# Window attention's norms and inverse roots: another division of work among the engines

## The chip, the cores and the metric

The kernel runs on one core of a Trainium2 chip. The metric is device time in microseconds (us) for one execution. The core's engines work side by side, each through its own queue in order: TensorE (PE in the profile; PEld are its weight loads), VectorE (DVE), ScalarE (ACT), GpSimd (POOL) and SyncE (SP), whose queue issues nearly all DMAs. They wait for each other through semaphores. All data is float32.

## What is computed

Two layers on an image batch x of 8 x 192 x 64 x 64, one behind the other. The first widens to 384 channels, convolves 3 x 3 by channel, runs a gated scan in four directions, normalises and returns to 192 channels. The second is attention in windows of 8 x 8 pixels with six heads of 32 channels, and an MLP. The change is in the second; its core, cut:

```python
def _layer_norm(x, g, b):
    mu = jnp.mean(x, -1, keepdims=True)
    var = jnp.mean(jnp.square(x - mu), -1, keepdims=True)
    return (x - mu) * jax.lax.rsqrt(var + EPS_LN) * g + b      # EPS_LN = 1e-5
...
shortcut = _layer_norm(xs, norm1_g, norm1_b)
...
qkv = (xin @ qkv_w.T + qkv_b).reshape(B_, N, 3, HEADS, HEAD_DIM)
...
attn = jnp.einsum('bhnd,bhmd->bhnm', _l2n(q), _l2n(k)) * temperature
kth = jax.lax.top_k(attn, IN_CC)[0][..., -1:]
attn = jnp.where(attn >= kth, attn, NEG)
...
attn = jax.nn.softmax(attn + rpb[None], axis=-1)
out = jnp.einsum('bhnm,bhmd->bhnd', attn, v)
...
out = out @ proj_w.T + proj_b
...
x2 = shortcut + out
hdn = _layer_norm(x2, norm2_g, norm2_b)
hdn = jax.nn.gelu(hdn @ fc1_w.T + fc1_b, approximate=False) @ fc2_w.T + fc2_b
x2 = x2 + hdn
```

The residual is the normalised input: the sum behind the attention adds `shortcut` (`xin` is its window layout), not the layer's input. `_l2n` divides by the length of a vector. So each token needs three inverse square roots: of the variance at the first norm, of the squared lengths of q and k (twelve heads' worth), and of the variance at the second norm.

## The kernel before

**Tiling.** An image is cut into 8 rows of windows ("window rows", `g`) of 8 x 64 = 512 tokens, and these into four blocks of 128 tokens, tokens on partitions, 192 channels along the free axis. There are 64 window rows in all (8 images of 8). The first layer works on 384 channels as three tiles (`ct`) of 128 partitions and, in the scan, on 512 pixels at each of 8 steps `t`, for 4 directions and 3 channel tiles: 12 tiles a step.

**Order.** The kernel does not issue in the order of its source. Generators write down steps (`plan(engine, cost, function, r=..., w=...)`), each with an estimated cost and the tiles it reads and writes. `Plan.order` then simulates the queues `RUNS` times, moving each step's rank towards the time when its result is needed, and keeps the shortest of these schedules. `SLACK` (ns) is how late an input may be for a step to be still picked by its rank. The engines' queues are filled in the chosen order, which is fixed from then on. Three strands lie side by side: `front` (first layer's convolution of the next image), `scan` (of this image), `window_row` (attention of the image before). The first image's convolution runs ahead of the plan, from a separate piece of code (lines 477 to 502), and the attention of the last image can start only when its scan and the statistics behind it are done (`scales`, line 1135).

**A window row** (line 1141 on): `zg` is loaded and scaled (1171); `tokens` (1186) multiplies it with `w_out`, whose columns have been freed of their mean, so that its result needs no mean for the first norm. VectorE multiplies by the gain `n1_g` into `s0` (1193), ScalarE sums the squares (1205), POOL scales and adds epsilon (1211), and `rsqrt` (613 to 620) makes the inverse root: Ln, Exp and Square on ScalarE, then a Newton step of three POOL instructions. This happens for two blocks at a time, twice a row. ScalarE scales `s0` (1219), PE transposes it into `sT` (1151), and from `sT` come q, k (1236) and v (1275). `nn` holds the squared lengths; it has the same `rsqrt` (one call for all four blocks) and scales q and k (1310). Scores, the search for the top entries, the mask and the softmax follow (1351 to 1437).

Behind the attention, again for two blocks at a time, `projected` (1506) multiplies with `w_pr`; VectorE adds `s0` (1518) and takes mean and variance with batch-norm instructions (1529, 1530); POOL adds epsilon (1536), `rsqrt` follows, and `less_m` = -mean x root is made on ScalarE and POOL (1546, 1553). ScalarE writes the normalised `xn` (1561), PE transposes it (1574, 1576), and the MLP follows: `widened` (1593, 1597), Gelu (1613), `narrowed` (1627).

**Other lines that are spoken of.** `scales` (1130 to 1135) is a run of tiny VectorE instructions on tiles of SBUF behind each image's scan. The mask (1392) and the scaling of q and k (1310) are VectorE instructions with two inputs in SBUF. GpSimd's large instructions in the scan are lines 896, 913, 917, 928, 981, 987 and 989.

## Time and profile before

| | |
|---|---|
| three runs | 7535.86, 7552.91, 7554.57 us; median 7552.91 |
| profiled execution | 7551.0 us; span of its instructions 7549.2 us |
| busy: PE, DVE, POOL, ACT | 6680.5 (88%), 6360.6 (84%), 6227.8 (82%), 4895.1 us (65%) |
| mean granted TensorE clock | 0.864 of full speed |
| end of the images' scans (line 1135) | 955, 1822, 2663, 3549, 4439, 5337, 6188, 7036 us |
| Gelu instructions before the scan's last gate instruction | 54 of 64 |

"Busy" is the time in which an engine had an instruction in work, also when that instruction stood still for something inside it. In a group's line the numbers behind the bar are the group's busy time in us and the mean of one instruction in ns, then the engine's idle time ahead of the group with what ended it. In a timeline a line gives start and duration in us. The DMA share is 0.2 to 0.6 in all stretches.

### The profile page before, as it was taken

The numbers are of one execution on the slowest core, as the hardware profiler recorded it, in microseconds if no ns is written. First come the engines' busy times: TensorE is split into PE (matmuls) and PEld (weight loads), VectorE is DVE, ScalarE is ACT, GpSimd is POOL, SyncE is SP. The second block draws the span as 40 slices with busy tenths as digits, with TensorE's granted clock in tenths as the row PEclk, the third lists the DMA queues.
The fourth block names the chain that finished last, engine by engine and source line by source line (L and its number), as shares of the span: only waits on it lengthen the run. The fifth ranks groups of instructions, "written<-read, shape, count | busy, mean of one in ns | idle before, by whom it ended". The sixth has DMA issues, their size and how long they took to land. (4 is left out here: it accounts for less than half of the span.)

```text
span 7549.2 us, 141750 instructions
## 1 busy us (share of the span) xinstructions
PE 6680.5 (88%) x50180; PEld 3448.8 (46%) x50180; DVE 6360.6 (84%) x15477; ACT 4895.1 (65%) x9649; POOL 6227.8 (82%) x6333
## 2 busy tenths in 40 slices
PE   7888799898989899888999899989888888898887
PEld 3333344444444444444445444444444444444554
DVE  6787798988899889898898988889899988899543
ACT  3555377765676567675777757776666656666765
POOL 1898788998899989987988888889899989899422
PEclk8887699987988889898988889987888878888999
DMA  5666354313541246213641144411121121111110
GB/s 165 163 174 162 108 154 124 81 50 100 157 120 50 68 133 158 65 49 94 162 117 44 53 121 132 119 47 53 54 55 48 45 67 44 50 45 45 32 22 14
DMA packets 988330, 669.39 MB, mean 89 GB/s; under 512 B 651971, under 2 KB 814214, under 8 KB 987622
## 3 DMA queue, kind: packets, MB, share of 16 engines
q1 hardware_dynamic: 986486, 658.87, 32.5%
q8 instruction: 398, 6.52, 0.4%
q14 instruction: 310, 2.54, 0.1%
q10 hardware_dynamic: 1136, 1.47, 0.1%
HBM read 433.98 MB, written 226.18 MB: 87 GB/s over the span
## 5 line engine op out<-in xcount | busy, mean ns | idle before, releaser
L808 PE MATMUL g<-xe,w_g 32*128 32x512 f32 x3648 | 1165.2, 749 | 228.5 <-DVE dx L967 80.5
L808 PE MATMUL g<-xo,w_g 32*128 32x512 f32 x3648 | 1201.7, 730 | 186.3 <-DVE dx L967 95.6
L865 ACT ACTIVATE ab<-g 128x512 f32<-128x512 f32 x1344 | 784.9, 596 | 397.9 <-PE nb L808 169.6
L896 POOL TENSOR_TENSOR ab<-ab 128x512 f32<-128x512 f32 x672 | 866.0, 1289 | 163.1 <-ACT ab L865 151.5
L928 POOL TENSOR_TENSOR pw<-pw,rr 128x512 f32<-128x512 f32 x672 | 865.9, 1289 | 134.7 <-ACT rr L911 113.7
L913 POOL TENSOR_TENSOR pw<-pw,pq 128x512 f32<-128x512 f32 x672 | 881.6, 1312 | 77.7 <-DVE pq L872 52.0
L917 POOL TENSOR_TENSOR pw<-pw,pq 128x512 f32<-128x512 f32 x672 | 877.4, 1306 | 15.5
L909 ACT ACTIVATE rr<-nb,eps 128x512 f32<-128x512 f32 x672 | 461.9, 687 | 577.9 <-DVE nb L906 575.3
L981 POOL TENSOR_TENSOR dx<-dx,hu 128x512 f32<-128x512 f32 x576 | 743.0, 1298 | 111.0 <-DVE hu L972 94.2
L808 PEld LDWEIGHTS g<-xo,w_g 32*128 32x128 f32 x3648 | 412.8, 207 | 726.8 <-DVE dx L967 200.3
L808 PEld LDWEIGHTS g<-xe,w_g 32*128 32x128 f32 x3648 | 407.2, 212 | 702.9 <-DVE dx L967 179.4
L1627 PE MATMUL lp<-hd,w_f 128*64 128x256 f32 (+1 forms) x2304 | 604.7, 502 | 57.2 <-ACT hd L1613 15.0
L989 POOL TENSOR_TENSOR y<-y,dx 128x512 f32<-128x512 f32 x384 | 598.2, 1565 | 2.2
L695 PE MATMUL lp<-strip,w_cv 128*32 128x256 f32 x8064 | 566.8, 420 | 27.3 <-DMA strip<-pad 22.7
L924 DVE SCALAR_TENSOR_TENSOR nb<-nb,rr 128x512 f32<-128x512 f32 x672 | 464.0, 691 | 145.4 <-ACT rr L911 142.8
L933 DVE SCALAR_TENSOR_TENSOR nb<-nb,pw 128x512 f32<-128x512 f32 x672 | 463.6, 690 | 139.3 <-POOL pw L928 137.4
L906 DVE TENSOR_TENSOR nb<-nb,ab 128x512 f32<-128x512 f32 x672 | 464.1, 691 | 115.1 <-POOL ab L896 106.6
L972 DVE TENSOR_TENSOR hu<-g,hid 128x512 f32<-128x512 f32 x768 | 516.8, 678 | 0.9 <-PE g L808 0.6
L887 ACT ACTIVATE nb<-nb 128x512 f32<-128x512 f32 x672 | 399.5, 595 | 141.1 <-DVE pq L874 80.3
L808 PE MATMUL nb<-xe,w_g 32*128 32x512 f32 x672 | 479.1, 799 | 10.0 <-DVE hid L941 9.8
L808 PE MATMUL nb<-xo,w_g 32*128 32x512 f32 x672 | 464.1, 777 | 16.9 <-DVE hid L941 16.8
L941 DVE TENSOR_TENSOR hid<-lx,nb 128x512 f32<-128x512 f32 x672 | 454.2, 676 | 4.9
(223 smaller groups left out, 16413.8 us busy)
## 6 DMA issues: line engine op xcount, KB each, us to landing
strip<-pad SPq DMA_DIRECT2D x1008, 132.0 KB
xd<-xsT SPq DMA_DIRECT2D x384, 256.0 KB
x<-xs SPq DMA_DIRECT2D x64, 768.0 KB
xd<-xs SPq DMA_DIRECT2D x192, 256.0 KB
z<-y SPq DMA_DIRECT2D x64, 768.0 KB
zg<-z SPq DMA_DIRECT2D x64, 768.0 KB
pad<-xin SPq DMA_DIRECT2D x168, 264.0 KB
xsT<-sn SPq DMA_DIRECT2D x168, 256.0 KB
```

The lines of the kernel that those rows point to most:

```text
L695: nc.tensor.matmul(pc()[q * RG : (q + 1) * RG, k * 256 : (k + 1) * 256].rearrange("p (h w) -> p h w", h=4), lhsT=w_cv[:, ct, q, dx, :], rh ...
L808: nc.tensor.matmul(dst, lhsT=w[rows, col : col + P], rhs=xp[rows, :], start=True, stop=True)
L865: lambda r=r: nc.scalar.activation(ab()[:, r, :], g[r](), AF.Abs),
L896: plan("POOL", gp(512), lambda: nc.gpsimd.tensor_add(ab()[:, 0, :], ab()[:, 0, :], ab()[:, 1, :]), w=[ab])
L906: plan("DVE", vec(512), lambda: nc.vector.tensor_add(nb(), nb(), ab()[:, 0, :]), r=[ab], w=[nb])
L913: plan("POOL", gp(512), lambda: nc.gpsimd.tensor_add(one(), one(), pq()[:, 0, :]), r=[(pq, 0)], w=[pw])
L917: lambda: nc.gpsimd.tensor_add(one(), one(), pq()[:, 1, :]),
L928: plan("POOL", gp(512), lambda: nc.gpsimd.tensor_mul(one(), one(), rr()), r=[rr], w=[pw])
L972: lambda: nc.vector.tensor_mul(like(hu(), d), like(pu(), d), state(d, ct)),
L981: plan("POOL", gp(512), lambda: nc.gpsimd.tensor_add(dx(), dx(), hu()), r=[hu], w=[dx])
L989: nc.gpsimd.tensor_add(y, y, dx().rearrange("p (c i) -> p i c", c=CH))
L1627: nc.tensor.matmul(dst[:, at : at + rhs.shape[-1]], lhsT=lhsT, rhs=rhs, **flags)
```

## The change

The text of the changed parts, cut (unchanged neighbours as context):

```diff
-    RUNS = 60
-    SLACK = 40.0
+    RUNS = 9
+    SLACK = 20
...
-                s.rank = (s.rank + rank) / 2 if n else rank
+                s.rank = 0.4 * s.rank + 0.6 * rank if n else rank
...
-        by_vector = [(ct, u) for ct, u in units if ct < CT - 1 or u == 0]
+        by_vector = [(ct, u) for ct, u in units if ct < CT - 1]
...
-            if n in (4, 6, 7):
-                convolved_by_products(CT - 1, (4, 6, 7).index(n) + 1)
+            if n in (2, 4, 5, 6):
+                convolved_by_products(CT - 1, (2, 4, 5, 6).index(n))
```

```diff
-    def rsqrt(v, key, shape, name, gain=1.0):
+    def rsqrt(v, key, shape, name, gain=1.0, mean=1.0, eps=0.0):
...
-        plan("ACT", tiny, lambda: nc.scalar.activation(r(), v(), AF.Ln), r=[key], w=[r])
+        more = {"bias": {1e-5: eps5}[eps]} if eps else {}
+        plan("ACT", tiny, lambda: nc.scalar.activation(r(), v(), AF.Ln, scale=1.0 / mean, **more), r=[key], w=[r])
         plan("ACT", tiny, lambda: nc.scalar.activation(r(), r(), AF.Exp, scale=-0.5, bias=log_c[gain]), w=[r])
-        plan("ACT", tiny, lambda: nc.scalar.activation(sq(), r(), AF.Square), r=[r], w=[sq])
+        plan("ACT", tiny, lambda: nc.scalar.activation(sq(), r(), AF.Square, scale=mean**-0.5), r=[r], w=[sq])
         def newton():
-            nc.gpsimd.tensor_mul(v(), v(), sq())
-            nc.gpsimd.tensor_scalar(v(), v(), -1.0, 3.0 * c * c, ALU.mult, ALU.add)
-            nc.gpsimd.tensor_mul(v(), v(), r())
+            nc.vector.scalar_tensor_tensor(v(), v(), eps * mean, sq(), ALU.add, ALU.mult)
+            nc.vector.scalar_tensor_tensor(v(), v(), 3.0 * c * c, r(), ALU.subtract, ALU.mult)
-        plan("POOL", (750.0, 60.0), newton, r=[r, sq], w=[key])
+        plan("DVE", (160.0 + 4 * math.prod(shape[1:]) / 0.96, 85.0), newton, r=[r, sq], w=[key])
```

The root comes out with its sign turned; the weights that follow it (`w_qk`, `w_v`, `w_f1`, and `w_dg` below) are turned too, once, ahead of the plan. The gain `n1_g` goes into `w_qk` and `w_v` there as well, so `s0` and `sT` hold the norm without its gain, and the multiplication of line 1193 becomes a ScalarE copy:

```diff
             plan(
-                "DVE",
-                vec(2 * DM),
-                lambda two=two, pz=pz: nc.vector.tensor_mul(
-                    s0()[:, two, :],
-                    pz()[:, 0 : 2 * DM].rearrange("p (k m) -> p k m", k=2),
-                    n1_g.unsqueeze(1).to_broadcast([P, 2, DM]),
+                "ACT",
+                act(2 * DM),
+                lambda two=two, pz=pz: nc.scalar.copy(
+                    s0()[:, two, :], pz()[:, 0 : 2 * DM].rearrange("p (k m) -> p k m", k=2)
                 ),
...
-            plan(
-                "POOL",
-                tiny,
-                lambda ss=ss: nc.gpsimd.tensor_scalar(ss(), ss(), 1.0 / DM, 1e-5, ALU.mult, ALU.add),
-                w=[ss],
-            )
-            rsqrt(ss, ss, [P, 2], "ss")
...
+        rsqrt(ss, ss, [P, NT], "ss", mean=DM, eps=1e-5)
```

Behind the attention the residual is added by TensorE into the same PSUM bank, from `sT` with the small diagonal matrix `w_dg` (96 x 97, the gain on its diagonal, and a column that yields minus the mean); `w_pr` has a 193rd column for the mean, too. ScalarE copies the sum out, takes minus the mean, and sums the squares of what is left:

```diff
+                    for j in range(2):
+                        cols = slice(at + j * HALF, at + j * HALF + more)
+                        nc.tensor.matmul(pp()[:, cols], lhsT=sT[:, j, tok], rhs=w_dg[:, j, :], start=False, stop=j == 1)
...
+            def unfolded(t2=t2, pp=pp):
+                nc.scalar.copy(
+                    x2()[:, 2 * t2 : 2 * t2 + 2, :].rearrange("p k (j m) -> p k j m", j=2),
+                    bass.AP(pp().tensor, pp().offset, [pp().ap[0], [DM + 1, 2], [HALF + 1, 2], [1, HALF]]),
+                )
+            plan("ACT", act(2 * DM), unfolded, r=[pp], w=[(x2, t2)])
...
+                lambda pp=pp, two=slice(2 * t2, 2 * t2 + 2): nc.scalar.copy(less_m()[:, two], view(pp(), [[DM + 1, 2]], HALF)),
...
+            def spread(t2=t2):
+                for k in range(2 * t2, 2 * t2 + 2):
                     nc.scalar.activation(
-                        xn()[:, tt, :], x2()[:, tt, :], AF.Identity, bias=less_m()[:, k : k + 1], scale=sd()[:, k : k + 1]
+                        xn()[:, k, :], x2()[:, k, :], AF.Square, bias=less_m()[:, k : k + 1], accum_out=sd()[:, k : k + 1]
                     )
...
+        rsqrt(sd, sd, [P, NT], "sd", mean=DM, eps=1e-5)
+        plan("DVE", (70.0, 85.0), lambda: nc.vector.tensor_mul(less_m(), less_m(), sd()), r=[sd], w=[less_m])
```

The batch-norm instructions, the addition of line 1518 and the POOL steps of lines 1536 and 1553 are gone. Each of the two norms now has one root for all four blocks of a window row, where it had two for two blocks each. `sT` is kept twice (by the row's parity), since it is read until the projection; `s0`, `st` and `acc_p` have one buffer where they had two. No DMA is added or taken away, but for the shapes of three small loads.

More of the change, by code (lines that the diff above doesn't have):

```diff
@@ L387, in tile_ss2d_then_window_attention @@
     w_pr = load("w_pr", rows=P)
-    n1_g = load("n1_g", a["n1_g"].partition_broadcast(P))
+    n1_g = load("n1_g")
     n1_b = load("n1_b")
@@ L413, in tile_ss2d_then_window_attention @@
     xT = blank("xT", [P, 2, GT])
-    sT, oT = (blank(n, [P, 2, GT], 0.0) for n in ("sT", "oT"))
-    for t in (sT, oT):
+    sTs, oT = [blank(f"sT{k}", [P, 2, GT], 0.0) for k in range(2)], blank("oT", [P, 2, GT], 0.0)
+    w_dg = blank("w_dg", [P, 2, HALF + 1], 0.0)
+    for t in (*sTs, oT):
         nc.gpsimd.memset(t[HALF : HALF + 1, 1, :], 1.0)
@@ L482, in convolved_by_products @@
         def convolved_by_products(ct, u):
-            acc = epool.tile([P, 16, W], F32, name="acc_p", bufs=2)
+            acc = epool.tile([P, 16, W], F32, name="acc_p", bufs=1)
             for k in range(2):
@@ L559, in tile_ss2d_then_window_attention @@
         bias_row("b_pr", w_pr, [(b_v[:, j : j + 1], w_pr[0:HALF, j, :]) for j in range(2)], "n1_br")
+        msum = prep.tile([P, 2], F32, name="msum")
+        nc.vector.tensor_reduce(msum, w_pr, AX.X, ALU.add, negate=True)
+        nc.vector.tensor_scalar(w_pr[:, :, HALF], msum, 1.0 / DM, None, ALU.mult)
+        for j in range(2):
+            own, mean = (slice(0, HALF), HALF) if j == 0 else (slice(1, HALF + 1), 0)
+            gain = n1_g[:, j : j + 1]
+            nc.vector.tensor_scalar(gain, gain, -1.0, None, ALU.mult)
+            nc.vector.tensor_scalar(w_dg[0:HALF, j, own], ident[0:HALF, 0:HALF], gain, None, ALU.mult)
+            nc.vector.tensor_scalar(w_dg[0:HALF, j, mean : mean + 1], gain, -1.0 / DM, None, ALU.mult)
+            for w in (w_qk[0:HALF, j, :], w_v[0:HALF, j, :]):
+                nc.vector.tensor_scalar(w, w, gain, None, ALU.mult)
         ps = prep_ps.tile([P, 512], F32, name="ps_pre")
@@ L570, in tile_ss2d_then_window_attention @@
             w = w_f1[:, ci, :]
-            nc.vector.tensor_scalar(w, w, n2_g[:, ci : ci + 1], None, ALU.mult)
+            nc.vector.tensor_scalar(w, w, n2_g[:, ci : ci + 1], -1.0, ALU.mult, ALU.mult)
         top_b = prep.tile([P, 3], F32, name="top_b")
@@ L704, in convolve @@
             rows = slice(s * 64, (s + 1) * 64)
-            st = Held(fpool, [P, CH, 64], "st", bufs=2)
+            st = Held(fpool, [P, CH, 64], "st", bufs=1)
             plan(
@@ L1114, in scan @@
         rsqrt(gr, gr, [P, CT], "gr")
-        plan("DVE", tiny, lambda: nc.vector.tensor_mul(gn(), gn(), gr()), r=[gr], w=[gn])
+        plan("DVE", tiny, lambda: nc.vector.scalar_tensor_tensor(gn(), gn(), -1.0, gr(), ALU.mult, ALU.mult), r=[gr], w=[gn])
         pg = bank()
@@ L1153, in turn @@
                         )
-                plan("PE", turned(4), turn, r=[src], w=[pt])
+                plan("PE", turned(4), turn, r=[src], w=[pt, (key, "room")])
                 plan(
@@ L1162, in two_blocks @@
                 )
+        sT, kS = sTs[g % 2], f"sT{g % 2}"
         zg = Held(lpool, [P, CT, CH, 64], "zg", bufs=1)
@@ L1173, in window_row @@
         plan("ACT", (2116.0, 102.0), scaled_up, r=[sc, bb], w=[zg])
-        s0 = Held(lpool, [P, NT, DM], "s0", bufs=2)
+        s0 = Held(lpool, [P, NT, DM], "s0", bufs=1)
+        ss = Held(small, [P, NT], "ss")
         for t2 in range(2):
             pz = bank()
-            ss = Held(small, [P, 2], "ss")
             for k in range(2):
@@ L1200, in window_row, with squares, scaled @@
             )
-            def squares(pz=pz, ss=ss):
+            def squares(t2=t2, pz=pz):
                 for k in range(2):
                     part = pz()[:, k * DM : (k + 1) * DM]
-                    nc.scalar.activation(part, part, AF.Square, accum_out=ss()[:, k : k + 1])
-            plan("ACT", (782.0, 100.0), squares, w=[pz, ss])
-            plan(
-                "POOL",
-                tiny,
-                lambda ss=ss: nc.gpsimd.tensor_scalar(ss(), ss(), 1.0 / DM, 1e-5, ALU.mult, ALU.add),
-                w=[ss],
-            )
-            rsqrt(ss, ss, [P, 2], "ss")
-            def scaled(t2=t2, ss=ss):
-                for k in range(2):
-                    part = s0()[:, 2 * t2 + k, :]
+                    at = 2 * t2 + k
+                    nc.scalar.activation(part, part, AF.Square, accum_out=ss()[:, at : at + 1])
+            plan("ACT", (782.0, 100.0), squares, w=[pz, (ss, t2)])
+            yield
+        rsqrt(ss, ss, [P, NT], "ss", mean=DM, eps=1e-5)
+        for t2 in range(2):
+            def scaled(t2=t2):
+                for k in range(2 * t2, 2 * t2 + 2):
+                    part = s0()[:, k, :]
                     nc.scalar.activation(part, part, AF.Copy, scale=ss()[:, k : k + 1])
             plan("ACT", (694.0, 106.0), scaled, r=[ss], w=[(s0, t2)])
-            yield
+        yield
         plan.lane = 7
-        two_blocks(sT, "sT", s0)
+        two_blocks(sT, kS, s0)
         yield
@@ L1238, in projected @@
                     )
-            plan("PE", mm(2, DIN), projected, r=["sT"], w=[pq, (qk, "room")])
+            plan("PE", mm(2, DIN), projected, r=[kS], w=[pq, (qk, "room")])
             plan(
@@ L1281, in values @@
                         )
-            plan("PE", mm(4, DM), values, r=["sT"], w=[pv, (v, "room")])
+            plan("PE", mm(4, DM), values, r=[kS], w=[pv, (v, "room")])
             plan(
@@ L1496, in window_row @@
         x2, xn = (Held(lpool, [P, NT, DM], n, bufs=1) for n in ("x2", "xn"))
+        less_m, sd = Held(small, [P, NT], "less_m"), Held(small, [P, NT], "sd")
         for t2 in range(2):
@@ L1499, in window_row, with projected @@
             two = slice(2 * t2, 2 * t2 + 2)
-            stats, mv, sd = Held(small, [P, 2, 6], "stats"), Held(small, [P, 2, 2], "mv"), Held(small, [P, 2], "sd")
-            def projected(t2=t2, pp=pp):
+            more = HALF + 1
+            def projected(t2=t2, pp=pp, sT=sT):
                 for k in range(2):
                     tok = slice((2 * t2 + k) * P, (2 * t2 + k + 1) * P)
+                    at = k * (DM + 1)
                     for j in range(2):
                         nc.tensor.matmul(
-                            pp()[:, k * DM : (k + 1) * DM],
-                            lhsT=oT[:, j, tok],
-                            rhs=w_pr[:, j, :],
-                            start=j == 0,
-                            stop=j == 1,
-                        )
@@ L1514, in window_row @@
-            plan("PE", mm(4, DM), projected, r=["oT"], w=[pp, (x2, "room"), (xn, "room")])
-            plan(
-                "DVE",
-                vec(2 * DM),
-                lambda two=two, pp=pp: nc.vector.tensor_add(
-                    x2()[:, two, :].rearrange("p k m -> p (k m)"),
-                    pp()[:, 0 : 2 * DM],
-                    s0()[:, two, :].rearrange("p k m -> p (k m)"),
-                ),
-                r=[pp, s0],
-                w=[(x2, t2)],
-            )
@@ L1527, in moments @@
-            def moments(t2=t2, stats=stats, mv=mv):
-                for k in range(2):
-                    nc.vector.bn_stats(stats()[:, k, :], x2()[:, 2 * t2 + k, :])
-                    nc.vector.bn_aggr(mv()[:, k, :], stats()[:, k, :])
-            plan("DVE", (947.0, 83.0), moments, r=[(x2, t2)], w=[stats, mv])
-            plan(
-                "POOL",
-                tiny,
-                lambda mv=mv, sd=sd: nc.gpsimd.tensor_scalar(sd(), mv()[:, :, 1], 1e-5, 1.0, ALU.add, ALU.mult),
-                r=[mv],
-                w=[sd],
-            )
@@ L1540, in window_row @@
-            rsqrt(sd, sd, [P, 2], "sd")
-            less_m = Held(small, [P, 2], "less_m")
+                            pp()[:, at : at + DM + 1], lhsT=oT[:, j, tok], rhs=w_pr[:, j, :], start=j == 0, stop=False
+                        )
+                    for j in range(2):
+                        cols = slice(at + j * HALF, at + j * HALF + more)
+                        nc.tensor.matmul(pp()[:, cols], lhsT=sT[:, j, tok], rhs=w_dg[:, j, :], start=False, stop=j == 1)
+            plan("PE", mm(6, 2 * (DM + HALF + 2) / 3), projected, r=["oT", kS], w=[pp, (x2, "room"), (xn, "room")])
@@ L1545, in window_row, with normed @@
                 tiny,
-                lambda mv=mv, less_m=less_m: nc.scalar.activation(less_m(), mv()[:, :, 0], AF.Copy, scale=-1.0),
-                r=[mv],
-                w=[less_m],
-            )
-            plan(
-                "POOL",
-                tiny,
-                lambda sd=sd, less_m=less_m: nc.gpsimd.tensor_mul(less_m(), less_m(), sd()),
-                r=[sd],
-                w=[less_m],
-            )
-            def normed(t2=t2, less_m=less_m, sd=sd):
-                for k in range(2):
-                    tt = 2 * t2 + k
-                    nc.scalar.activation(
-                        xn()[:, tt, :], x2()[:, tt, :], AF.Identity, bias=less_m()[:, k : k + 1], scale=sd()[:, k : k + 1]
+                lambda pp=pp, two=slice(2 * t2, 2 * t2 + 2): nc.scalar.copy(less_m()[:, two], view(pp(), [[DM + 1, 2]], HALF)),
+                r=[pp],
+                w=[(less_m, t2)],
+            )
+            def spread(t2=t2):
+                for k in range(2 * t2, 2 * t2 + 2):
+                    nc.scalar.activation(
+                        xn()[:, k, :], x2()[:, k, :], AF.Square, bias=less_m()[:, k : k + 1], accum_out=sd()[:, k : k + 1]
+                    )
+            plan("ACT", (782.0, 100.0), spread, r=[(x2, t2), (less_m, t2)], w=[(xn, t2), (sd, t2)])
+            yield
+        rsqrt(sd, sd, [P, NT], "sd", mean=DM, eps=1e-5)
+        plan("DVE", (70.0, 85.0), lambda: nc.vector.tensor_mul(less_m(), less_m(), sd()), r=[sd], w=[less_m])
+        for t2 in range(2):
+            def normed(t2=t2):
+                for k in range(2 * t2, 2 * t2 + 2):
+                    nc.scalar.activation(
+                        xn()[:, k, :], x2()[:, k, :], AF.Identity, bias=less_m()[:, k : k + 1], scale=sd()[:, k : k + 1]
                     )
             plan("ACT", (890.0, 95.0), normed, r=[(x2, t2), less_m, sd], w=[(xn, t2)])
-            yield
+        yield
         for ci in range(2):
@@ L1698, in _laid_out @@
     cols = lambda a, n: np.ascontiguousarray(a.reshape(-1, n).T)
+    gap = lambda a: np.concatenate([a[..., :HALF], np.zeros_like(a[..., :1]), a[..., HALF:]], -1)
     L0, L1 = "L0_conv_", "L1_conv_"
@@ L1740, in _laid_out @@
         "b_v": cols(qkv_b[2].reshape(DM), HALF),
-        "w_pr": rows(proj.reshape(DM, DM), HALF),
-        "b_pr": f(L1 + "proj_b").reshape(1, DM),
-        "n1_g": f(L1 + "norm1_g"),
-        "n1_br": f(L1 + "norm1_b").reshape(1, DM),
+        "w_pr": gap(rows(proj.reshape(DM, DM), HALF)),
+        "b_pr": gap(f(L1 + "proj_b").reshape(1, DM)),
+        "n1_g": cols(f(L1 + "norm1_g"), HALF),
+        "n1_br": gap(f(L1 + "norm1_b").reshape(1, DM)),
         "n1_b": cols(f(L1 + "norm1_b"), HALF),
```

## The prediction

> **What bounds the kernel now.** I read first the busy times by stretch, cut where the eight batches end (a batch ends with its line 1135, at 955, 1822 ... 7036 us), then the chain of waits, then the groups of instructions, last the instructions of single lines.

> ```profile
> core 0: us, PE busy (x) PEld busy (x) DVE busy (x) ACT busy (x) POOL busy (x), PEclk, DMA share, GB/s
> ...
> 4439.00:5337.00 898.00, 821.93 (x6494) 432.23 (x6490) 787.47 (x1922) 606.40 (x1205) 777.31 (x787) 0.87 0.35 92
> 5337.00:6188.00 851.00, 743.97 (x5156) 396.30 (x5156) 781.39 (x1927) 564.51 (x1139) 778.87 (x789) 0.84 0.19 52
> 6188.00:7036.00 848.00, 731.19 (x5237) 391.05 (x5238) 763.39 (x1986) 571.34 (x1172) 749.01 (x785) 0.86 0.17 47
> 7036.00:7549.00 513.00, 432.09 (x3961) 273.64 (x3959) 225.47 (x1134) 323.39 (x688) 146.62 (x317) 0.92 0.09 20
> ```

> The reader is to see three engines level. In the sixth scanned batch DVE and POOL are busy 92% each and PE 87%; in the one before, which also has the next batch's convolution, PE is at 92%. Only behind 7036, where the last attention rows run alone, is PE far ahead of the rest. ACT is never above 70%.

> ```profile
> PE 8%; DVE 7%; POOL 4%; ACT 4%; issue 1%; DMA 0%; SPq 0%; POOLq 0%; ACTq 0%; DVEq 0%
> ```

> The chain can be followed back to 5780 us. Adding its pieces up by engine, from 5780 to 7036 they are DVE 34.0%, PE 25.2%, POOL 21.7%, ACT 12.1%; from 7036 on PE 50%, ACT 27%, DVE 15%, POOL 5%. I use these shares as weights: work added to an engine lengthens its stage by the share times the engine's growth. This assumes that the last batch and a half stand for all, a choice that I come back to.

> **The change, part by part.** VectorE loses four groups (their busy time is the first number behind the bar):

> ```profile
> L1193 DVE TENSOR_TENSOR s<-lp,n_g 128x384 f32<-128x384 f32 x128 | 69.6, 545 | 11.4 <-PE lp L1186 11.4
> L1518 DVE TENSOR_TENSOR x<-lp,s 128x384 f32<-128x384 f32 x128 | 69.6, 545 | 33.6 <-PE lp L1506 33.5
> L1529 DVE BATCH_NORM_STATS2 stats<-x 128x6 f32<-128x192 f32 x256 | 86.5, 338 | 0.6
> L1530 DVE BATCH_NORM_AGGREGATE mv<-stats 128x2 f32<-128x6 f32 x256 | 46.5, 182 | 8.9
> ```

> 272 us, 4.25 us for each of 64 rows. It gains seven small operations a row: two Newton steps for each of ss, sd and nn, and less_m times sd. They read two tensors of SBUF, and what such an operation costs here depends on GpSimd:

> ```profile
> 1816.44 1.18 DVE L1131 TENSOR_TENSOR sc<-sc,vecs 128x3 f32<-128x3 f32 x1
> 1817.66 1.45 DVE L1132 TENSOR_SCALAR sc<-sc 128x3 f32<-128x3 f32 x1
> 1819.14 1.43 DVE L1133 TENSOR_TENSOR bb<-sc,vecs 128x3 f32<-128x3 f32 x1
> ...
> 1816.33 1.27 POOL L913 TENSOR_TENSOR pw<-pw,pq 128x512 f32<-128x512 f32 x1
> 1817.55 3.00 POOL L989 TENSOR_TENSOR y<-y,dx 128x512 f32<-128x512 f32 x2
> ```

> Three elements take 1.2 to 1.45 us, and each ends within 0.1 us of a POOL instruction's end. With POOL idle the same line takes 0.164 us (its shortest of eight). Big ones show it too: line 1392 has a median of 0.97 us in the last two scanned batches and 0.66 behind 7036, where POOL rests; line 1310 2.23 against 1.76. The removed four have a PSUM operand or a single input and show no such wait.

> So the price, from rows: the first of a run takes 0.17 plus the mean excess of 1392 and 1310, 0.39: 0.56 us. One that follows at once meets a POOL instruction just begun: mean of lines 1131 to 1134, 0.96 us. A row has three firsts and four followers, 3 x 0.56 + 4 x 0.96 = 5.5 us while a scan runs, and 7 x 0.17 = 1.2 us behind the last scan. 56 x 5.5 + 8 x 1.2 + 12 (the same steps for gr, eight times) = 330 us; net **+58 us, +0.9%** of DVE's 6360.6. Bounds: all bare, 80 us, net -192 (-3.0%); all as line 1132 (1.16), 484 us, net +212 (+3.3%). I stay between, as POOL is busy some 90% of a batch.

> [...]

> POOL loses lines 618 to 620 (for ss 82.9, sd 76.9, nn 52.1 us), 1211 (26.0), 1536 (28.1), 1553 (25.4) and gr's (5): **-296 us, -4.75%**. VectorE's waits for ScalarE's Square now stand in VectorE's queue (51 us of idle time in POOL's before), with the scan's products queued behind them and PE waiting for these; against that go the 55 us of idle time ahead of the removed DVE groups. I set the two equal.

> TensorE gains, per row, eight products w_dg x sT of 97 columns, each two passes: 16 passes. A pass of 192 columns (line 1506, 16 in 2.87 us) takes 179 ns, one of 128 columns behind a 128-column load (line 1627, x2 against ident, 8 in 1.05 us) 131. The load does not shrink with 97 columns, so I take 131, with 99 (scaled by columns) and 179 as bounds: 16 x 0.131 = 2.1 us a row, **+134 us, +2.0%** (1.5 to 2.7%). The 193rd column of the other products is nothing. [...]

> ScalarE gains four copies of 384 columns (line 1287: 485 ns), four squares with a sum (between 509, line 1205 with its accumulator read, and 728, line 1561's 536 plus the same read; 728, as they too read SBUF and a bias), and loses six small operations (203, 292, 201 ns, twice): 1.94 + 2.91 - 1.39 = 3.5 us a row, **+221 us, +4.5%** (3.4% with 509).

> Weighted over the stretch from 955 to 7036 (6081 us): 0.340 x 0.9 - 0.217 x 4.75 + 0.252 x 2.0 + 0.121 x 4.5 = +0.34%, **+20 us**.

> Start: VectorE does nine convolution units of 11.3 us in a row (0.81 + 8 x 1.3, up to 116.5 us), now eight; the ninth goes to PE and ACT, which idle there. The folding of the norm's gain adds some 3 us of small operations behind it: **-8 us**. If acc_p's single buffer holds PE up, that is hidden by the units left. st's single buffer makes a ScalarE copy wait for the store before; copies are 14.9 us apart in the median, so I count nothing (up to 5 us).

> Order: 54 of the 64 Gelu instructions stand before the scan's last gate instruction on ScalarE; in the new order 56 do. Two rows move into scanned batches. Behind 7036 nine rows' worth cost PE 48, DVE 25, ACT 36, POOL 16 us each; with the terms above (and 1.4 us of port waits on lines 1392 and 1310) 50, 27.6, 39.4 and 11.7, weighted 29 us: **+59 us** for two. At the end, the first row of the last batch needed 140 us from line 1171 to its Gelu (7037 to 7177), two older rows among it, and seven more came 50.4 us apart. Without the older rows I take 125 (105 to 140), and 1.3 us more a row by the end's weights: -15 + 10 = **-5 us**. x2's chain there loses its wait for the moments and gets the sum of squares instead.

> Sum: -8 + 20 + 59 - 5 = +66 us on the profiled 7551.0 us, which lies 2 below the median: **7617 us**.

> **Rivals.** *GpSimd's relief decides (faster).* In the stretch from 955 to 7036 POOL, freer by 4.75%, lets the seven operations through bare: DVE -3.0%, weighted sum -1.0%, -61 us, and the two rows fit into what came free: 7551 - 61 - 8 - 5 = 7477. For it: 193 of DVE's 652 us of idle time between 1000 and 7000 us end on POOL. Against it: POOL would still be busy over 85%. It decides where the seven average below 0.3 us (0.79 in my sum): 56 x 7 x 0.49 x 0.34 = 65 us is what the forecast lies above the old time.

> *VectorE or TensorE alone sets the pace (much slower).* All seven at 1.16 us, wholly on the path: 7551 + 212 - 8 = 7755. Or PE: 56 x 2.1 + 2 x 48 - 8 - 5 = +201, 7752. For it: PE's 92% with the convolution; DVE ends most of PE's idle time (337 of 603 us in the same stretch). Against PE: its granted clock rises where it is fuller (0.94 at 95% busy from 2750 to 3000 us, 0.73 at 76% from 750 to 1000), so filled gaps pay part.

> *It does not do what it says.* What moves is the planner's order (9 rounds for 60, slack 20 for 40), which knows nothing of the port; works added and taken cancel: 7551, give or take 20.

> **How the numbers follow.** Forecast 0.45 (7575 to 7700), GpSimd 0.28 (7400 to 7540), one engine alone 0.14 (7700 to 7800), cancelling 0.13. The three runs before lie 0.25% apart, so 0.3%, 23 us, is what can be told from no change. Faster 0.30, same 0.13, slower 0.57. Range 7430 to 7770, the forecast's own 7575 to 7700.

> **What would show it.** The two Newton lines and less_m's product: right if they average 0.6 to 1.1 us before the last batch ends and under 0.25 behind it; wrong below 0.3. POOL's busy sum near 5930, PE's near 6810, ACT's near 5115, DVE's near 6410. Passes w_dg x sT near 131 ns apart. First DVE work behind the convolutions 11 us earlier. Last batch's end near 500 us from its scales. It is wrong if the batches, with eight rows each, take less than 850 us.

## The result, and the profile after

The changed kernel takes 7593.74 us in the median of five runs (7579.65 to 7601.64), the kernel before 7548.15, also of five (7535.86 to 7554.57): a ratio of 1.0056, interval 1.004 to 1.0072. That is 46 us slower. The profiled execution took 7583.05 us, 32 more than the one before.

The busy times by stretch, with the same columns as before, cut at the ends of the last scanned batches (6271 and 7132 us):

```profile
core 0: us, PE busy (x) PEld busy (x) DVE busy (x) ACT busy (x) POOL busy (x), PEclk, DMA share, GB/s
5392.00:6271.00 879.00, 761.36 (x5492) 411.35 (x5491) 801.78 (x1889) 587.89 (x1214) 743.24 (x618) 0.85 0.18 51
6271.00:7132.00 861.00, 740.25 (x5452) 405.30 (x5450) 779.77 (x1950) 602.54 (x1225) 719.24 (x601) 0.87 0.17 46
7132.00:7581.00 449.00, 379.69 (x3488) 246.47 (x3488) 187.88 (x960) 298.55 (x656) 91.22 (x112) 0.93 0.10 21
```

Before, VectorE and GpSimd stood level at 92% in the first of these stretches. Now GpSimd is at 85% and VectorE still at 91%, in a stretch 28 us longer. The page's chain of waits says the same; it now reaches back over some 35% of the span, and VectorE leads it:

```profile
DVE 13%; PE 11%; ACT 5%; POOL 3%; issue 2%; DMA 1%; ACTq 0%; SPq 0%; DVEq 0%; POOLq 0%
```

The new groups of VectorE, with the mean of one instruction in ns behind the comma:

```profile
L630 DVE SCALAR_TENSOR_TENSOR nn<-nn,nn_r 128x48 f32<-128x48 f32 x64 | 54.6, 854 | 2.2
L630 DVE SCALAR_TENSOR_TENSOR ss<-ss,ss_r 128x4 f32<-128x4 f32 x64 | 50.3, 786 | 2.2
L630 DVE SCALAR_TENSOR_TENSOR sd<-sd,sd_r 128x4 f32<-128x4 f32 x64 | 50.3, 786 | 2.2
L629 DVE SCALAR_TENSOR_TENSOR sd<-sd,sd_q 128x4 f32<-128x4 f32 x64 | 48.6, 759 | 45.9 <-ACT sd_q L626 45.8
...
L629 DVE SCALAR_TENSOR_TENSOR nn<-nn,nn_q 128x48 f32<-128x48 f32 x64 | 37.3, 583 | 13.6 <-ACT nn_q L626 8.2 <-POOL at L1443 3.8 <-POOL pw L938 1.0
L629 DVE SCALAR_TENSOR_TENSOR ss<-ss,ss_q 128x4 f32<-128x4 f32 x64 | 36.4, 569 | 17.0 <-ACT ss_q L626 17.0
L1547 DVE TENSOR_TENSOR less_m<-less_m,sd 128x4 f32<-128x4 f32 x64 | 30.8, 481 | 0.4
```

Together these seven groups are 308 us for 448 instructions on four or 48 elements. A timeline of VectorE, and of GpSimd at the same time (start and duration in us), shows one row's three:

```profile
6625.06 0.59 DVE L629 SCALAR_TENSOR_TENSOR sd<-sd,sd_q 128x4 f32<-128x4 f32 x1 [1.43 <-ACT sd_q L626]
6625.68 1.44 DVE L630 SCALAR_TENSOR_TENSOR sd<-sd,sd_r 128x4 f32<-128x4 f32 x1
6627.15 1.19 DVE L1547 TENSOR_TENSOR less_m<-less_m,sd 128x4 f32<-128x4 f32 x1
...
6624.32 1.30 POOL L927 TENSOR_TENSOR pw<-pw,pq 128x512 f32<-128x512 f32 x1
6625.56 1.53 POOL L999 TENSOR_TENSOR y<-y,dx 128x512 f32<-128x512 f32 x1
6627.04 1.28 POOL L938 TENSOR_TENSOR pw<-pw,rr 128x512 f32<-128x512 f32 x1
```

Each of the three ends when the GpSimd instruction beside it ends: 6625.65 beside 6625.62, 6627.12 beside 6627.09, 6628.34 beside 6628.32. The loss has this shape, but the same trace shows gains too. By stage, from the scales' times and the first instruction of the plan on PE:

| stage | before, us | after, us | difference |
|---|---|---|---|
| start, to the plan's first matmul | 132.7 | 123.1 | -9.6 |
| first scan, no attention beside it | 822.9 | 809.8 | -13.1 |
| seven scans with attention beside them | 6080.4 | 6198.8 | +118.4 |
| after the last scan | 513.2 | 449.6 | -63.6 |

The last two lines have not the same work in them: of the 64 window rows' Gelus, 54 start before the end of the last scan in the kernel before and 56 in the changed one, so two rows have moved from the last line to the one above it, as forecast.

### The profile page after: what moved, and what is told of

Its sections match the earlier page's. It is cut to its first block, busy times and chain, and to the rows that moved or that the text cites. A ratio compares the mean times of both kernels' runs of the same rounds, so it can differ in the third digit from the quotient of the medians.

```text
span 7581.3 us, 142641 instructions
## 1 busy us (share of the span) xinstructions
PE 6741.8 (89%) x51240; PEld 3534.1 (47%) x51240; DVE 6430.6 (85%) x15176; ACT 5030.1 (66%) x10035; POOL 5952.7 (79%) x4968
## 5 line engine op out<-in xcount | busy, mean ns | idle before, releaser
L818 PE MATMUL g<-xo,w_g 32*128 32x512 f32 x3648 | 1164.5, 725 | 200.2 <-DVE dx L977 98.5
L818 PE MATMUL g<-xe,w_g 32*128 32x512 f32 x3648 | 1121.2, 732 | 184.1 <-DVE dx L977 55.9
L818 PEld LDWEIGHTS g<-xo,w_g 32*128 32x128 f32 x3648 | 393.2, 205 | 716.1 <-DVE dx L977 196.4
L1618 PE MATMUL lp<-hd,w_f 128*64 128x256 f32 (+1 forms) x2304 | 644.2, 532 | 59.8 <-ACT hd L1604 50.0
L989 POOL TENSOR_TENSOR y<-hu,dx 128x512 f32<-128x512 f32 x192 | 245.1, 1285 | 307.1 <-DVE hu L982 174.5
L1618 PEld LDWEIGHTS lp<-hd,w_f 128*64 128x64 f32 (+1 forms) x2304 | 293.9, 184 | 408.5 <-issue 246.2
```

The lines of the kernel that those rows point to most:

```text
L818: nc.tensor.matmul(dst, lhsT=w[rows, col : col + P], rhs=xp[rows, :], start=True, stop=True)
L1618: nc.tensor.matmul(dst[:, at : at + rhs.shape[-1]], lhsT=lhsT, rhs=rhs, **flags)
```

## The experiments

Two theories stood against each other: that the small two-input operations stand still on VectorE and this gives the gain back, and that TensorE's and ScalarE's added work, or the planner's settings, make the loss. In kernels marked "same order" every instruction stands where it stood in the plan. Each ratio is to the kernel before as it ran beside that experiment (medians of 7549 to 7558 us), so a difference in us between two experiments is uncertain by some 10 us.

**The second SBUF input, taken away.** e4 puts the root and its square into a PSUM bank:

```diff
-        r, sq = Held(small, shape, name + "_r"), Held(small, shape, name + "_q")
+        both, n = bank(), math.prod(shape[1:])
+        tall = lambda k: both()[:, 64 * k : 64 * k + n].rearrange("p (a b) -> p a b", a=shape[1]) if len(shape) == 3 else both()[:, 64 * k : 64 * k + n]
+        r, sq = (lambda: tall(0)), (lambda: tall(1))
...
```

> The changed kernel with the root and its square (outputs of Exp and Square) in a PSUM bank, so that each Newton instruction on VectorE has one input in SBUF and one in PSUM, same count; planned anew. Theory (the wait is for the second SBUF input): the six groups fall from 0.57-0.85 to about 0.2 us each, DVE busy by about 200 us, the time by 65-95 us to 7500-7530, less what the bank costs the others (0-40 us). Rival (the wait is for GpSimd by any small VectorE instruction, or only their number counts): the groups stay above 0.5 us, time 7580-7620.

Measured 7551.05 us, ratio to the kernel before 1.0001 (0.9992 to 1.0011): 43 us less than the changed kernel. The answers for its two Newton lines, with shortest, median and longest duration in ns:

```profile
L631 DVE SCALAR_TENSOR_TENSOR ss<-ss,lp x64: 105/147/159, 962.3 to 7372.6; 128x4 f32<-128x4 f32 x64
L631 DVE SCALAR_TENSOR_TENSOR sd<-sd,lp x64: 128/148/160, 1114.7 to 7500.3; 128x4 f32<-128x4 f32 x64
...
L632 DVE SCALAR_TENSOR_TENSOR ss<-ss,lp x64: 157/158/160, 962.4 to 7372.8; 128x4 f32<-128x4 f32 x64
L632 DVE SCALAR_TENSOR_TENSOR nn<-nn,lp x64: 203/203/206, 1001.2 to 7424.7; 128x48 f32<-128x48 f32 x64
```

None is longer than 206 ns, where the changed kernel's reach 3770. Same engine, same count, same arithmetic; only one input has left SBUF. In e4, 294 of the 400 Newton instructions begin while a GpSimd instruction is in work and end over 60 ns before it does; of the changed kernel's 464 small operations (the 448 and gr's 16) 3 do. That the wait belongs to the second SBUF input is shown. The gain is below the 65 to 95 us expected, by less than the 40 us allowed for the bank, and this kernel was planned anew, so not all of the 43 us need be the wait's.

**Two-input operations, doubled.** e5 and e6, same order, add two unused VectorE instructions behind each Newton step (`spare` is a small SBUF tile; the line that makes it is not shown):

```diff
+            for k in range(2):                                        # e5
+                nc.vector.scalar_tensor_tensor(spare[:, 2 + k], spare[:, 0], 0.5, spare[:, 1], ALU.add, ALU.mult)
+            for k in range(2):                                        # e6
+                nc.vector.reciprocal(spare[:, 2 + k], spare[:, 0])
```

> The changed kernel, same order, and behind each Newton step two more VectorE products of two small SBUF tensors that nothing uses (400 more in all). Theory (each stands still for GpSimd's current instruction): 0.7-0.9 us each, DVE busy +280 to +350, the time by the weights 0.34-0.46 up by 100 to 170, to 7695-7765. Rival (only the number of instructions counts): as e6.

> As e5, with two reciprocals of one small tensor in place of the products. Theory: about 0.2 us each without a wait, DVE busy +70 to +90, 7615-7645. Rival (only the number counts): the same time as e5.

e5 took 7740.92 us, ratio 1.0243 (1.0228 to 1.0258), e6 7618.94, ratio 1.0079 (1.0063 to 1.0094): 147 and 25 us more than the changed kernel for the same number of instructions. First e5's, then e6's:

```profile
L633 DVE SCALAR_TENSOR_TENSOR spare<-spare x400: 147/155/1591, 931.1 to 7704.6; 128x4 f32<-128x4 f32 x134
```

```profile
L633 DVE RECIPROCAL spare<-spare x400: 137/157/175, 929.0 to 7579.5; 128x4 f32<-128x4 f32 x134
```

The same median, but the products reach 1591 ns (mean 470) and the reciprocals never 176; 139 of these, too, begin and end inside a GpSimd instruction. The times were expected; the busy time was not. VectorE's grew by 139 us in e5, not 280 to 350: 287 of the 400 added products take under 0.35 us, so most slip in without a wait. Yet the time grew by 147: in this fixed order an added microsecond of VectorE cost 1.06 us, not the 0.34 or 0.46 of the chain's shares. e5's range held only because two errors cancelled. In e6 the busy time grew by 24 us where 70 to 90 had been expected; its 25 us of time are too few for a price, since its interval overlaps the changed kernel's.

**Newton steps moved alone.** e3 takes the kernel before, same order, and issues its five Newton steps a row on VectorE:

```diff
-            nc.gpsimd.tensor_mul(v(), v(), sq())
-            nc.gpsimd.tensor_scalar(v(), v(), -1.0, 3.0 * c * c, ALU.mult, ALU.add)
-            nc.gpsimd.tensor_mul(v(), v(), r())
+            nc.vector.scalar_tensor_tensor(v(), v(), -1.0, sq(), ALU.mult, ALU.mult)
+            nc.vector.scalar_tensor_tensor(v(), v(), 3.0 * c * c, r(), ALU.add, ALU.mult)
```

> The kernel before with every instruction where it stood, only the Newton steps (five a row, three GpSimd instructions each) issued as two on VectorE. Theory: ten small operations a row at about 0.69 us, DVE busy +440 us (+6.9%), POOL -217 (-3.5%): 0.34 x 6.9 - 0.22 x 3.5 = +1.6%, 7640-7690. Rival (GpSimd's relief counts, the small operations find room): 7480-7540.

Measured 7744.61 us, ratio 1.0257 (1.0242 to 1.0272), 196 us more: the direction of the theory, beyond its range. VectorE's busy time grew by 259 us, GpSimd's fell by 204. Whatever that relief bought, it was less than VectorE's added time cost; this run alone cannot part the two.

e1 does the reverse with the changed kernel, same order; e2 tells the planner of it:

```diff
-            nc.vector.scalar_tensor_tensor(v(), v(), eps * mean, sq(), ALU.add, ALU.mult)
-            nc.vector.scalar_tensor_tensor(v(), v(), 3.0 * c * c, r(), ALU.subtract, ALU.mult)
+            if eps:
+                nc.gpsimd.tensor_scalar(v(), v(), eps * mean, 1.0, ALU.add, ALU.mult)
+            nc.gpsimd.tensor_mul(v(), v(), sq())
+            nc.gpsimd.tensor_scalar(v(), v(), 1.0, -3.0 * c * c, ALU.mult, ALU.add)
+            nc.gpsimd.tensor_mul(v(), v(), r())
...
-        plan("DVE", (160.0 + 4 * math.prod(shape[1:]) / 0.96, 85.0), newton, r=[r, sq], w=[key])   # e2 alone
+        plan("POOL", (900.0, 60.0) if eps else (750.0, 60.0), newton, r=[r, sq], w=[key])
```

> The changed kernel with every instruction where it stood, only the Newton steps' two VectorE instructions issued as three or four on GpSimd (add epsilon times mean, product, affine, product). Theory (VectorE's small two-input operations stand still until GpSimd's current instruction ends, and VectorE is the engine that most often ends last): DVE busy falls by the six groups' 281 us to about 6150, POOL's rises by about 150, the time falls by 65 (weights 0.34 and 0.22) to 125 us (the changed kernel's own weights), to 7470-7530, below the kernel before. Rival (TensorE's and ScalarE's new work and the two rows moved make the loss): within 20 us of 7594. Rival (GpSimd's relief is what counts): above 7600.

> As e1, but the planner is told that the Newton steps are GpSimd's (900 ns, 750 without epsilon), so that it orders anew. Theory: as e1 give or take 30 us, 7450-7540. If order decides more than the engine: off from e1 by over 40 us.

e1: 7581.36 us, ratio 1.0047 (1.0032 to 1.0062), not to be told from the changed kernel and where the rival put it. e2: 7509.94 us, ratio 0.9948 (0.9931 to 0.9965), where the theory put it, but off from e1 by more than 40 us, the sign given for the order. Between the two stands nothing but the order of the same instructions: 71 us. Two groups of e1 say where its gain went (busy, mean, then the idle time ahead of them):

```profile
L1319 DVE TENSOR_TENSOR qk<-qk,nn 128x1536 f32<-128x1536 f32 x64 | 154.1, 2407 | 38.8 <-POOL nn L1311 38.6
L1550 DVE TENSOR_TENSOR less_m<-less_m,sd 128x4 f32<-128x4 f32 x64 | 54.5, 852 | 78.2 <-POOL sd L633 77.3
```

In the changed kernel these stood idle 4.6 and 0.4 us. VectorE got 213 us less to do and, between 1000 and 7000 us, waited 189 us more, 146 of them for GpSimd: its queue holds these instructions where the root was to be ready, and GpSimd finished it later. e1's time alone is therefore no sign that TensorE's and ScalarE's work makes the loss, as its rival had it.

**Newton steps left out.** e9, same order, leaves all Newton steps out, so that roots are never formed.

```diff
         def newton():
+            return
```

> The changed kernel, same order, with the Newton steps left out (ss, sd, nn and gr stay as the sums that they were; 400 VectorE instructions fewer, 285 us of busy time, and nothing in their place). If a microsecond of VectorE counts as much when taken away as it did when added (e5, e6: about 1 to 1): 7300-7360. If this fixed order has other chains just behind (e1: VectorE 213 us less busy, 13 us gained): 7480-7560.

Measured 7407.40 us, ratio 0.981 (0.9796 to 0.9825): 186 us less than the changed kernel for 239 us of VectorE, 0.78 to 1. Its time is between the two ranges. So this order does let VectorE's time be gained, and e1's gain, by the idle times above, was lost to GpSimd's new place in it. The price is not VectorE's alone: with the Newton steps also goes the wait of those that need the root (ScalarE's scaling of s0 waited 53 us for line 630 in the changed kernel).

**The planner.** e7 gives the changed kernel the old settings, e8 tells its planner the measured durations, e10 gives the kernel before the new settings, e11 gives e2 the old ones:

```diff
-    RUNS = 9                    # e7, e11; e10 the reverse
-    SLACK = 20
+    RUNS = 60
+    SLACK = 40.0
...
-                s.rank = 0.4 * s.rank + 0.6 * rank if n else rank
+                s.rank = (s.rank + rank) / 2 if n else rank
...
-        plan("DVE", (160.0 + 4 * math.prod(shape[1:]) / 0.96, 85.0), newton, r=[r, sq], w=[key])   # e8
+        plan("DVE", (1350.0, 85.0), newton, r=[r, sq], w=[key])
...
-        plan("DVE", (70.0, 85.0), lambda: nc.vector.tensor_mul(less_m(), less_m(), sd()), r=[sd], w=[less_m])   # e8
+        plan("DVE", (450.0, 85.0), lambda: nc.vector.tensor_mul(less_m(), less_m(), sd()), r=[sd], w=[less_m])
```

> The changed kernel with the planner's settings of before (60 rounds, slack 40, half and half). Theory (the small operations' waits and the added work make the loss, not the settings): within 40 us of 7594. Rival (the settings make it): 7500-7550.

> The changed kernel with the planner told what the trace shows of the new VectorE steps (1350 ns for a Newton step where it had 177 to 360, 450 for less_m's product where it had 70), so ordered anew. If a good part of the loss is an order made with wrong durations: 7530-7565. If the waits themselves make it: 7575-7610.

> The kernel before with the planner's settings of the change (9 rounds, slack 20, 0.4 and 0.6). If the settings are simply better, as they were for the changed kernel (47 us): 7490-7520. If which settings fit is a matter of the kernel: within 40 us of 7550, to either side.

> e2 (all of the change, the Newton steps on GpSimd, planned so) with the planner's settings of before. Theory (the norms' move to TensorE and ScalarE is worth something by itself): below 7548. If e2's gain was the settings': 7545-7580.

| kernel | old settings | new settings |
|---|---|---|
| before | 7548 | e10: 7686, ratio 1.0177 (1.016 to 1.0194) |
| changed | e7: 7641, ratio 1.0112 (1.009 to 1.0134) | 7594, ratio 1.0056 (1.004 to 1.0072) |
| changed, Newton steps planned on GpSimd | e11: 7477, ratio 0.9904 (0.989 to 0.9919) | e2: 7510, ratio 0.9948 (0.9931 to 0.9965) |

e8 took 7605.12 us, ratio 1.007 (1.0051 to 1.0088): right durations in the planner gained nothing. The settings are neither good nor bad in themselves: 138 us worse for the kernel before, 47 better for the changed one, 33 worse for e2. e7 and e10 both lie outside the 40 us that were expected. Read down the columns: under either settings the Newton steps cost more on VectorE than on GpSimd (164 and 84 us), and the rest of the change is a gain over the kernel before (71 and 176 us). The change as a whole has no sign of its own: it costs 93 us under the old settings and gains 92 under the new ones. The measured 46 us hold both the work and the settings, old to new. e11 beats both kernels.

e12 moves the last small product to GpSimd as well:

```diff
-        plan("DVE", (70.0, 85.0), lambda: nc.vector.tensor_mul(less_m(), less_m(), sd()), r=[sd], w=[less_m])
+        plan("POOL", (270.0, 60.0), lambda: nc.gpsimd.tensor_mul(less_m(), less_m(), sd()), r=[sd], w=[less_m])
```

> e2 with the last small two-input product, less_m times sd, on GpSimd too (planned so). Theory: VectorE loses 55 us of busy time and 40 us of waits for GpSimd ahead of it, GpSimd gains 13: 7470-7500. Rival (order noise): 7500-7530.

7503.73 us, ratio 0.9937 (0.9922 to 0.9952): 6 us below e2, not to be told from it, and inside the rival's range. VectorE lost 62 us of busy time and the time did not follow; with orders that differ by more than that, this decides nothing.

## Why the prediction came out right, point by point

**Direction and size.** 66 us were forecast, 46 measured between medians and 32 between the profiled executions. The wait named for it is shown by e4, e5 and e6, and to be rid of it is worth 43 us (e4), 84 (e2) or 164 (e11 against e7), each planned anew. That the whole came out slower by 46 is in part luck: +20 and +59 became +118, -5 became -64, the first scan's -13 had no term, and the plan's order, which had none either, is worth 33 to 138 us in the table above. Under one and the same setting the change costs 93 us or gains 92.

**The price of a small operation: right.** Forecast 0.79 us each while a scan runs, 318 us with the last rows; measured 0.73, and 308 us. All 266 of them that took over 0.35 us in the scanned batches end within 0.1 us of the end of a GpSimd instruction. The first of a pair was put at 0.56 and took 0.66, the second at 0.96 and took 0.87; less_m's product, priced as a second, took 0.53. Behind the last scan they take 0.38, not 0.17, and 17 of 56 end with one of the softmax's GpSimd instructions. What the prediction calls the port are these waits, of VectorE instructions with two inputs in SBUF; no run shows what in the chip makes them wait.

**Busy times.** VectorE +70 us where +58 was forecast (5930 and 6410 were named for GpSimd and VectorE; they are 5953 and 6431). TensorE grew by 61, not 134, ScalarE by 135, not 221. (The four products of the weighted sum add up to 0.32%, not 0.34%; the 20 us stand.) TensorE's and ScalarE's new instructions:

```profile
L1519 PE MATMUL lp<-w_dg,sT 128*128 128x97 f32 x1024 | 155.1, 276 | 0.0
...
L1540 ACT ACTIVATE xn<-x,less_m 128x192 f32<-128x192 f32 x256 | 114.7, 452 | 3.4 <-DMA out_dram<-ot 1.2
...
L1540 ACT ACTIVATION_READ_ACCUMULATOR xn<-x,less_m 128x1 f32 x256 | 49.6, 194 | 0.0
```

The square with its sum is 452 + 194 ns, between the two rows used as bounds and nearer to neither than 82 ns. The passes with w_dg start 102 ns apart in the mean (four from 7254.22 to 7254.63 us), where 131 was taken; by this they are some 104 us, and the 155 above count time in which a pass, 276 ns long in the mean, overlaps its neighbours. The row of 131 was misread: 1.05 us for eight passes holds the last one's whole 0.28 us, and by their starts those 128-column passes are 112 ns apart. That TensorE grew by less than 104 goes with its other groups: the two largest, of line 808 and now 818, took 81 us less, at a granted clock of 0.870 where it was 0.864.

**The scans with attention: the mis-sized terms.** They took 118 us more, where +20 (the work, by the chain's shares) and +59 (two rows) had been added up. VectorE's weight was 0.34. In a fixed order a microsecond of it cost 1.06 (e5) and 0.78 (e9). But the change was planned anew, and in pairs planned anew a microsecond taken from VectorE was worth 0.10 (e12 against e2), 0.19 (e4), 0.37 (e2) and 0.89 (e11 against e7), with the order's chance in each and, but in e4, work added to GpSimd: 0.34 lies among them and is not refuted. Of the 118 us some 54 go with the Newton steps' waits: in e4 and e2, which also have 56 rows before the end of the last scan, these seven scans take 6145 us each. The forecast's weights had put the waits at 81 us there (0.34 of the 3.9% between its bound with bare operations, -3.0%, and its +0.9%). So the rest was too small: with bare operations the sum had -61 and +59, about nothing, and e4 shows +64, though VectorE is 108 us and GpSimd 221 us less busy in these scans than in the kernel before, TensorE 70 and ScalarE 149 us more. Whether the rows' price, TensorE's and ScalarE's work, GpSimd's relief (weighted with 0.22, tested by no run alone) or the order makes these 64 us stays open.

**The end: the other mis-sized term.** -5 us forecast, -64 measured. The first row of the last batch needs 99 us from zg's scaling to its Gelu, not 125 (105 was the lower bound), and the rows come 47.0 us apart, not 50.4 + 1.3: 26 and 33 us of the miss. The stretch from the first to the last of these Gelus, before and after:

```profile
7177.00:7530.00 353.00, 294.19 (x2668) 184.84 (x2668) 151.04 (x758) 217.72 (x460) 98.12 (x213) 0.92 0.08 18
```

```profile
7233.00:7562.00 329.00, 286.84 (x2704) 183.66 (x2704) 135.79 (x712) 222.67 (x473) 66.90 (x82) 0.95 0.07 17
```

TensorE's idle time a row fell from 8.4 to 6.0 us, its granted clock rose from 0.92 to 0.95, and it was busy 41.0 us a row instead of 42.0, with more to do. The chain there had 12.6% on VectorE and 4.9% on GpSimd, and has 3.5% and nothing: the sum and the moments (lines 1518, 1529 and 1530) stood in it for 16.8 of the 353 us, GpSimd's steps for sd and less_m for 10.0. The runs bear out that the rows come closer: 44.5 to 48.6 us apart in the changed kernel and all its variants, under both settings, against 48.9 to 51.2 in the kernel before, e10 and e3. How much of the first row's gain is the shorter chain cannot be parted from the older rows ahead of it: its Gelu comes 100 to 101 us behind the last scan where no older row is left (the changed kernel, e2, e7, e12), 107 with one (e11), 141 with two (the kernel before) and 200 with three (e10). The shares of that stretch as weights had set TensorE's new work against the shorter chain and missed it.

**The start: right.** -8 forecast, -9.6 measured.

**The rivals.** GpSimd's relief did not decide: the operations took 0.73 us, not under 0.3. "One engine alone" priced VectorE at 1 to 1, as e5 shows it for a fixed order, but with 1.16 us an operation. The granted clock of its two stretches is a tendency alone: in the kernel before it was also 0.83 at 92% busy (4250 to 4500 us) and 0.96 at 89% (7000 to 7250); that filled gaps pay part was an estimate, which no run tests. That the planner's order moves the time was right, but "give or take 20" was too small by a factor of two to seven, and the sign of the whole change hangs on it.

**Still open.** What TensorE's and ScalarE's added work and the two moved rows cost by themselves was not tried, nor how much of e4's 43 us is order. Why e11's order is better than e2's was not looked into.

## What to carry to other kernels

Before moving small operations from GpSimd to VectorE, look at a tiny VectorE instruction with two SBUF inputs in the trace: if it takes as long as a GpSimd instruction (1.44 and 1.19 us beside 1.53 and 1.28 in the timeline above), the move is paid for in VectorE's queue (259 us more busy time in e3); keep them on GpSimd or let one input come from PSUM (0.206 us at most in e4). In a kernel whose order is planned, compare two versions under more than one setting of the planner, since order alone can be worth more than the change, and turned its sign here. A chain's share is a poor price: VectorE, busy 91%, cost 1.06 us for each microsecond added to a fixed order, and gave back between 0.10 and 0.89 for each one taken away when the order was planned anew.

The length of the wait went with GpSimd's instructions (the 266 ends within 0.1 us of theirs), not with one's own size: four elements took up to 3.77 us (line 629), and in e6 a reciprocal of the same four never more than 0.175 us. Nor does it always last for one instruction alone. The longest lay across three that follow each other without a gap (GpSimd's first, then VectorE's):

```profile
5831.20 1.51 POOL L999 TENSOR_TENSOR y<-y,dx 128x512 f32<-128x512 f32 x1
5832.68 1.27 POOL L938 TENSOR_TENSOR pw<-pw,rr 128x512 f32<-128x512 f32 x1
5833.92 1.26 POOL L906 TENSOR_TENSOR ab<-ab 128x512 f32<-128x512 f32 x1
```

```profile
5831.42 3.77 DVE L629 SCALAR_TENSOR_TENSOR sd<-sd,sd_q 128x4 f32<-128x4 f32 x1 [0.22 <-ACT sd_q L626]
```

One more of the 464 lay across two (2.15 us at 5631.15). Why these two waited longer is not known.

Behind loads of 128 columns, passes of 97 columns (line 1519) and of 128 (line 1618, x against ident) start 111 and 112 ns apart in the median; passes of 193 columns (line 1514) 167. So the 31 columns fewer bought next to nothing.
